# One tile in sixteen takes its source rows from columns copied on chip instead of a row gather

## The chip, the cores and the metric

The kernel runs on one core of a Trainium2 chip. A core has a matrix engine (PE, with its weight loads shown apart as PEld), a vector engine (DVE), a scalar engine (ACT), a general engine (POOL, GpSimd), an engine that only issues transfers (SP, SyncE), and 16 DMA engines. Each engine works through its own list of instructions in order; the order of the five lists is written out by hand here. The metric is the device time of one execution in microseconds (us), the median of several runs.

## The reference

One message-passing layer on a graph: 12,500 nodes with 64 features, 200,000 edges sorted by destination, 32 features per edge.

```python
msg_in = jnp.concatenate([nodes[row], nodes[col], edge_features], axis=-1)
messages = relu(msg_in @ mW1 + mb1) @ mW2 + mb2
aggregated = jax.ops.segment_sum(messages, col, num_segments=nodes.shape[0])
upd_in = jnp.concatenate([nodes, aggregated], axis=-1)
x = _layernorm(x + relu(upd_in @ uW1 + ub1) @ uW2 + ub2)
```

`row` is the source of an edge, in no order; `col` is its destination, in ascending order. All is fp32.

## The kernel before

**Tables.** The product of `msg_in` with `mW1` splits in three: a part of the source node, a part of the destination node and a part of the edge. The first two depend on a node alone, so two tables in DRAM hold them for every node: `tab_a` for sources and `tab_b` (with the bias) for destinations, 128 numbers per node. `chunk_a` and `chunk_b` compute them, most of `tab_a` before the loop.

**Tiles, groups, steps.** The edges are cut in 1563 tiles of 128. Eight tiles are a group (the kernel's `s`, 196 of them), and one pass of the main loop (lines 583 to 622) is one step; two groups share an index `g` and a set of selection matrices. A group's first linear layer is a PSUM bank pair `pc` of 128 x 1024.

**What one step does**, in the program's order, each on its own engine:

- `gather` (line 153) on POOL, for a group up to 14 steps ahead: eight indirect transfers (line 164), one per tile, each fetching 128 rows of `tab_a` by the edges' sources into a row buffer. There are `ROWB` = 14 row buffers; `frees` tells which step's end makes room. The first `XG` = 8 groups, when the table is not complete, gather rows of `x` instead and go through `transpose` and a matmul with `w1a`.
- `windows` (line 213) on SP: eight transfers of 32 consecutive rows of `tab_b` into `rhs`, at a row number that SP reads into a register. Because the edges are sorted, the 128 destinations of a tile lie within 32 nodes.
- `node_part` (line 255): DVE adds the gathered rows to `pc` (line 272), then ACT applies the relu in place (line 273), giving `h`. The add is the last reader of the row buffer; POOL's next gather into this buffer waits for it.
- `collect` (line 283) on PE, for the group before: the messages are summed per destination by a matmul of each tile's `h` with a 32-column selection matrix, into the PSUM tile `sums` at a column from a register (line 298), and likewise the counts of edges (line 303).
- `select`, `counts`, `load`, `loadd` once per two groups: DVE builds the selection matrices `l` (line 192) and `sel` (line 196), ACT makes a bf16 copy of the latter (line 204), SP loads destinations (line 180) and edge features (line 211).
- `edge_part` (line 242) on PE, for the next group: eight matmuls (line 251) of [edge features; selection] with [weights; 32 rows of `tab_b`] into `pc`. They wait for the `rhs` transfers and for the DVE add that frees `pc`, of which there are two.
- every three or four steps a node update of 384 nodes (`close`, `columns`, `carry`, `update`, `residual`, `norm`, `store`).

The order of the DVE's list in a step is: add of line 272, then on every second step lines 190, 192 and 196. ACT's is: relu of line 273, then on every second step line 204.

Of the kernel before, what the change touches and what calls it, by code (L numbers as in the profile page):

```python
# [10 lines left out]
F32 = mybir.dt.float32  # L11
I32 = mybir.dt.int32
AF = mybir.ActivationFunctionType
ALU = mybir.AluOpType
# [3 lines left out]
P = 128  # L18
# [6 lines left out]
SUB = 8  # L25
# [15 lines left out]
EARLY = NCH * P  # L41
GE = 20
BS = 8
UB = 3
NCOL = (-(-N // P) + UB) * P
UW = UB * P
# [16 lines left out]


@with_exitstack
def gnn_kernel(ctx: ExitStack, tc: tile.TileContext, x1T, x, eT, e_rows, src, dst, dst_row, wrow, wnext, whalf,
               mW1, mb1, mW2, mb2, uW1, ub1, uW2, ub2, out):

# [35 lines left out]
    past = const.tile([1, 1], F32, name="past")  # L104
    w1b = const.tile([P, DH], F32, name="w1b")
    b1 = const.tile([P, DH], F32, name="b1")

    sums_s = [const.tile([P, UW], F32, name=f"sums_s{k}") for k in range(2)]
    xw = [const.tile([P, UW], F32, name=f"xw{k}") for k in range(2)]
# [21 lines left out]
    cps = cpool.tile([P, WIN + SUP], F32, name="cps")  # L131
    slot = cps[:, :WIN]
    drc = const.tile([P, NT], F32, name="drc")
    flag_i = const.tile([1, 1], I32, name="flag_i")
    usup = const.tile([1, K], I32, name="usup")
    ustep = const.tile([1, K], I32, name="ustep")
# [4 lines left out]

    rows = ctx.enter_context(tc.tile_pool(name="rows", bufs=ROWB))
    xg = {}

    def frees(s):

# [3 lines left out]
    def tiles(s):  # L150
        return range(s * SUB, min((s + 1) * SUB, NT))

    def gather(s):

        if s >= XG or s % 2 == 0:
            buf = rows.tile([P, SUB, DH], F32, name="xg")
        else:
            buf = xg[s - 1][0]
        if s < XG:
            a = buf.rearrange("p k (b d) -> p (k b) d", d=D)[:, s % 2 * SUB:(s % 2 + 1) * SUB, :]  # L160
        else:
            a = buf.rearrange("p (b k) d -> p k b d", b=2)
        for i, t in enumerate(tiles(s)):
            nc.gpsimd.indirect_dma_start(  # L164
                out=a[:, i, :] if s < XG else a[:, i // 2, i % 2, :], out_offset=None, in_=A[:, :] if s >= XG else x[:, :],
                in_offset=bass.IndirectOffsetOnAxis(ap=src_s[:, t:t + 1], axis=0))
        xg[s] = buf, a

    with tc.tile_pool(name="sup", bufs=2) as sup, tc.tile_pool(name="work", bufs=2) as work, tc.manual_schedule():
# [63 lines left out]
            nc.scalar.copy(xt, pt)  # L233
            xs[s] = xt

        def parts(n):

            if n == SUB:
                return [slice(0, SUB)]
            return [slice(b * SUB // 2, b * SUB // 2 + (n - b + 1) // 2) for b in range(2) if n > b]  # L240

        def edge_part(s):

            n = len(tiles(s))
            g, j = divmod(s, SUP // SUB)
            pc = psum.tile([P, 2, SUB // 2, DH], F32, name="pc")
            for i in range(n):
                k, b = divmod(i, 2)
                q, m = 64 * b, j * SUB // 2 + k

                nc.tensor.matmul(pc[:, b, k, :], L[g][q:q + 64, m, :], rhs[g % 2][q:q + 64, m, :],  # L251
                                 start=s >= XG or k == 0, stop=s >= XG)
            pcs[s] = pc

        def node_part(s):

            n = len(tiles(s))
            pc = pcs.pop(s)
            h = work.tile([P, 2, SUB // 2, DH], F32, name="h")
            if s < XG:  # L260
                xt = xs.pop(s)
                for i in range(n):
                    k, b = divmod(i, 2)
                    q = 64 * b
                    nc.tensor.matmul(pc[:, b, k, :], xt[q:q + 64, k, :], w1a[q:q + 64], start=False,
                                     stop=i + 2 >= n)
                nc.scalar.activation(h, pc, AF.Relu)
            else:
                hf, pf = (t.rearrange("p b k f -> p (b k) f") for t in (h, pc))
                a = xg.pop(s)[0]  # L270
                for m in parts(n):
                    nc.vector.tensor_tensor(hf[:, m], pf[:, m], a[:, m], op=ALU.add)  # L272
                    nc.scalar.activation(hf[:, m], hf[:, m], AF.Relu)  # L273
            hs[s] = h

        def opened(u):
# [37 lines left out]
        def close(u):  # L314

            ps, pn = sums.pop(u)
            nc.scalar.copy(sums_s[u % 2], ps)  # L317
            nc.scalar.copy(xw[u % 2][0:1], pn)

        us = {}  # L320

# [46 lines left out]
            nc.sync.dma_start(out[bass.ds(n0, UW), :].rearrange("(c p) d -> p c d", p=P), o)  # L368


        WCH = 1024

        def relative(a, b):

# [108 lines left out]
        for k, c in enumerate(range(0, NB, NCH)):  # L483
            chunk_a(c)
            if k == 0:
                chunk_b(0, [B0v, Bv])
            if k == 2:

                w0 = wint[:, :GE * SUP]
                nc.vector.tensor_scalar(past, w0[:, GE * SUP - 1:], float(EARLY - WIN), None, op0=ALU.is_gt)  # L490
                nc.vector.tensor_scalar(w0, w0, float(EARLY - WIN), None, op0=ALU.min)
                windows(0)
                windows(1)
            if k == 4:
                relative(0, 8 * SUP)
            if k == 6:
                offsets()
            if k == 9:
                select(0)
                load(0)  # L500
                counts(0)
        columns_of(NCH, nc.sync)

        def rest(s):

            if s == 1:
                relative(8 * SUP, 8 * SUP + WCH)
            elif s == 2:
                relative(8 * SUP + WCH, NT)
# [73 lines left out]
        for s in range(last + 3):  # L583
# [18 lines left out]
            if chunks and s >= BS and chunks[0] < NCH + NB * (s + 1 - BS) / (SUP // SUB * (GE - 1) - BS):  # L602
                if len(chunks) > 1:
                    columns_of(chunks[1], nc.sync)
                chunk_b(chunks.pop(0), [Bv])
            if s + 1 < NSUB:
                if s + 1 < XG:
                    transpose(s + 1)
                edge_part(s + 1)
# [179 lines left out]
```

## Time and profile before

| | |
|---|---|
| median of 3 runs | 2791.69 us |
| lowest, highest | 2774.48 us, 2797.45 us |
| the profiled execution | 2797.45 us, of which its span 2795.7 us |
| POOL busy | 1476.6 us (53%), 1572 instructions |
| PE matmuls busy, weight loads busy | 1650.0 us (59%), 1427.7 us (51%) |
| DVE busy | 553.1 us (20%), 1103 instructions |
| ACT busy | 361.6 us (13%), 534 instructions |
| DMA traffic | 213.70 MB, mean 76 GB/s |
| gathers of `tab_a` by POOL | 1499, of 64 KB each |

A line of the profile's list of groups reads: line, engine, operation, written tile <- read tiles, number | busy us, mean ns of one | idle time of the engine just before them, and what ended it. A line of the timeline reads: start, duration, engine, line, operation, and in brackets the engine's idle time before it and what ended it. "issue" means that the profile shows nothing that was waited for; "remote" that a semaphore was waited for whose writer the profile does not name. SPq is SP's list of transfers.

### The profile page before, as it was taken

What the parts mean: (1) busy time and instruction counts of PE and PEld (TensorE: products, weight loads), DVE (VectorE), ACT (ScalarE), POOL (GpSimd) and SP (SyncE); (2) the same over time, 40 slices, a digit from 0 to 9 for tenths busy, and PEclk for the clock granted to TensorE, in tenths of its full rate; (3) what the DMA queues carried; (4) which work ended last, traced back from release to release, by engine and by line L of the source; (5) the groups of instructions that cost most, each with busy time, mean ns of one, the idle gap of its engine ahead of it and who ended that gap; (6) DMA issues with size and microseconds to landing.
All of it is one profiled execution on the core that took longest, in us unless ns stands there. A gap on an engine that the chain in (4) does not pass through costs nothing. (4 is left out here: it accounts for less than half of the span.)

```text
span 2795.7 us, 34750 instructions
## 1 busy us (share of the span) xinstructions
PE 1650.0 (59%) x9558; PEld 1427.7 (51%) x9558; DVE 553.1 (20%) x1103; ACT 361.6 (13%) x534; POOL 1476.6 (53%) x1572
## 2 busy tenths in 40 slices
PE   1412755555564646655656655656666676675788
PEld 1312654555454545544546544555555555564667
DVE  0200121222111112111211211212122222221233
ACT  0100101101010111111111111111111111111122
POOL 7175445654555655555555564565555555555510
PEclk6555555555555555555555555555555555555566
DMA  3531233333222222222222222222222222222221
GB/s 89 144 90 51 74 84 91 90 93 85 69 75 67 78 67 73 74 72 72 74 73 74 73 75 71 70 77 76 71 76 66 77 75 75 75 78 73 74 69 44
DMA packets 248063, 213.70 MB, mean 76 GB/s; under 512 B 81153, under 2 KB 213143, under 8 KB 247880
## 3 DMA queue, kind: packets, MB, share of 16 engines
q0 software_dynamic: 50016, 100.44, 14.0%
q1 hardware_dynamic: 182310, 100.72, 13.1%
q10 hardware_dynamic: 15554, 10.31, 1.3%
q8 instruction: 90, 1.47, 0.2%
q14 instruction: 93, 0.76, 0.1%
HBM read 192.55 MB, written 18.68 MB: 76 GB/s over the span
## 5 line engine op out<-in xcount | busy, mean ns | idle before, releaser
L164 POOL DMA_INDIRECT xg<-tab_a,src_s x1499 | 1415.0, 944 | 1183.8 <-DVE h L272 440.6
L251 PE MATMUL pc<-rhs,l 64*128 64x128 f32 x3126 | 531.4, 424 | 677.5 <-issue 411.8
L251 PEld LDWEIGHTS pc<-rhs,l 64*128 64x128 f32 x3126 | 432.1, 306 | 733.9 <-issue 629.4
L298 PEld LDWEIGHTS sums<-sel,h 128*128 128x128 f32 x3126 | 637.2, 301 | 206.6 <-issue 199.8
L298 PE MATMUL sums<-sel,h 128*128 128x32 f32 x3126 | 626.8, 366 | 151.7 <-issue 149.8
L272 DVE TENSOR_TENSOR h<-pc,xg 128x1024 f32<-128x1024 f32 x189 | 228.6, 1210 | 954.5 <-remote 319.5
L273 ACT ACTIVATE h<-h 128x1024 f32<-128x1024 f32 x189 | 197.7, 1047 | 598.9 <-DVE h L272 495.3
L196 DVE TENSOR_TENSOR sel<-cps,drc 128x512 f32<-128x512 f32 x98 | 67.3, 686 | 634.6 <-remote 333.4
L192 DVE TENSOR_TENSOR l<-l,cps 128x1024 f32<-128x1024 int32 (+1 forms) x101 | 123.3, 1221 | 206.0 <-DMA l<-in_dst_row 159.6
L204 ACT CAST selb<-sel 128x512 bf16<-128x512 f32 x98 | 60.4, 616 | 667.4 <-DVE sel L196 398.4
L303 PE MATMUL cnt<-selb,one 128*1 128x32 bf16 x1563 | 95.2, 188 | 51.0 <-issue 50.6
L336 ACT ACTIVATE hTu<-pu,ub_s 128x384 f32<-128x384 f32 x54 | 31.3, 580 | 696.0 <-remote 308.5
L344 PE MATMUL py<-ux,xw 128*128 128x64 f32 x324 | 95.5, 384 | 26.7 <-issue 23.1
L303 PEld LDWEIGHTS <-one 128*1 128x1 bf16 x1563 | 62.7, 83 | 89.7 <-issue 77.5
L345 PE MATMUL py<-u,hTu 128*128 128x64 f32 x324 | 93.9, 382 | 21.1 <-issue 20.7
L344 PEld LDWEIGHTS py<-ux,xw 128*128 128x128 f32 x324 | 77.1, 288 | 34.3 <-issue 28.4
L345 PEld LDWEIGHTS py<-u,hTu 128*128 128x128 f32 x324 | 79.8, 297 | 26.0 <-issue 25.5
L408 PE MATMUL pb<-w1a,xl 64*128 64x128 f32 x196 | 30.6, 430 | 99.6 <-DMA xl<-in_x1T 93.2
L333 PE MATMUL pu<-sums_s,w2u 128*128 128x384 f32 x108 | 88.2, 921 | 1.5 <-ACT sums_s L317 1.5
L408 PEld LDWEIGHTS pb<-w1a,xl 64*128 64x128 f32 x196 | 26.2, 311 | 103.7 <-issue 92.8
L334 PE MATMUL pu<-xw,uz 128*128 128x384 f32 x108 | 73.7, 782 | 0.0
L349 DVE BATCH_NORM_STATS2 st<-py 128x6 f32<-128x64 f32 x162 | 26.6, 220 | 237.6 <-PE py L345 120.3
(86 smaller groups left out, 594.3 us busy)
## 6 DMA issues: line engine op xcount, KB each, us to landing
l<-in_dst_row SPq DMA_DIRECT2D x196, 128.0 KB
l<-in_eT SPq DMA_DIRECT2D x196, 128.0 KB
rhs<-tab_b SPq DMA_DIRECT2D x1563, 16.0 KB
xg<-tab_a,src_s POOLq DMA_INDIRECT x1499
tab_b<-tb SPq DMA_DIRECT2D x13, 512.0 KB
tab_a<-tb ACTq DMA_DIRECT2D x12, 512.0 KB
xw<-in_x1T SPq DMA_DIRECT2D x54, 97.5 KB
out<-o SPq DMA_DIRECT2D x54, 96.0 KB
```

The lines of the kernel that those rows point to most:

```text
L164: nc.gpsimd.indirect_dma_start(out=a[:, i, :] if s < XG else a[:, i // 2, i % 2, :], out_offset=None, in_=A[:, :] if s >= XG else x[:, :], ...
L192: nc.vector.tensor_tensor(l[r], l[r].bitcast(I32), node[r].unsqueeze(2).broadcast_to([r.stop - r.start, SUP // 2, P]), op=ALU.is_equal)
L196: nc.vector.tensor_tensor(s[:, :nt], slot.unsqueeze(1).broadcast_to([P, nt, WIN]), drc[:, g * SUP:g * SUP + nt].unsqueeze(2).broadcast_to( ...
L251: nc.tensor.matmul(pc[:, b, k, :], L[g][q:q + 64, m, :], rhs[g % 2][q:q + 64, m, :], start=s >= XG or k == 0, stop=s >= XG)
L272: nc.vector.tensor_tensor(hf[:, m], pf[:, m], a[:, m], op=ALU.add)
L273: nc.scalar.activation(hf[:, m], hf[:, m], AF.Relu)
L298: nc.tensor.matmul(ps[:, bass.ds(ws[i], WIN)], h[:, i % 2, i // 2, :], S[g][:, k0 + i, :], start=False, stop=ends and i == n - 1)
L303: nc.tensor.matmul(pn[:, bass.ds(ws[i], WIN)], one, SB[g][:, k0 + i, :], start=False, stop=ends and i == n - 1)
L333: nc.tensor.matmul(pu, w2u, sums_s[u % 2], start=True, stop=False)
L334: nc.tensor.matmul(pu, uz, xw[u % 2], start=False, stop=True)
L344: nc.tensor.matmul(py[:, i], xw[u % 2][:, i * P:(i + 1) * P], ux, start=True, stop=False)
L345: nc.tensor.matmul(py[:, i], hT[:, i * P:(i + 1) * P], u2, start=False, stop=True)
```

## The change

From group 12 on, in every second group, the last of the eight tiles is no longer gathered. Its source rows of `x` come from a copy of the transposed `x` that is kept in SBUF (`xcol`, features on 64 partitions, one column per node): for each of the tile's 128 edges one column of 64 numbers is copied into a tile `xo`, at a column number read into a register, and one more matmul with `w1a` adds that tile's source part to `pc`. The 128 columns are copied in two consecutive steps, 64 in each: 36 by ACT, 28 by DVE. The DVE's copies are written as an addition of a column of zeros in PSUM. So 91 of the 1499 gathers go; 11,648 column copies come, with as many register instructions, and 91 matmuls. `xcol` is loaded before the loop by seven transfers on SP (3.2 MB), `srow` (the sources, a tile per row) in step 2. In the groups concerned, the DVE add covers seven tiles, and ACT applies the relu of the eighth straight from PSUM.

In the main loop `copies(s)` stands after `select`, `load`, `counts`, `loadd` and `chunk_b` and before `edge_part(s + 1)`; a tile `xo` is filled in an even and the following odd step, and `edge_part` reads it in the step after these.

```diff
+CG = 2
+CF = 6 * CG
+CA = 36
+NCT = -(-(NSUB - CF) // CG)
...
+    xcol = const.tile([P, NB * P], F32, name="xcol")
...
+    srow = const.tile([NCT, P], I32, name="srow")
+    xo = [const.tile([P, P], F32, name=f"xo{k}") for k in range(2)]
...
+    def copied(s):
+        return s >= CF and s % CG == CG - 1 and len(tiles(s)) == SUB
...
-        for i, t in enumerate(tiles(s)):
+        for i, t in enumerate(tiles(s)[:SUB - copied(s)]):
...
+                c = copied(s) and i == n - 1
                 nc.tensor.matmul(pc[:, b, k, :], L[g][q:q + 64, m, :], rhs[g % 2][q:q + 64, m, :],
-                                 start=s >= XG or k == 0, stop=s >= XG)
+                                 start=s >= XG or k == 0, stop=s >= XG and not c)
+                if c:
+                    nc.tensor.matmul(pc[:, b, k, :], xo[s // CG % 2][q:q + 64], w1a[q:q + 64], start=False, stop=True)
...
-                for m in parts(n):
+                for m in parts(n, copied(s)):
                     nc.vector.tensor_tensor(hf[:, m], pf[:, m], a[:, m], op=ALU.add)
                     nc.scalar.activation(hf[:, m], hf[:, m], AF.Relu)
+                if copied(s):
+                    nc.scalar.activation(h[:, 1, SUB // 2 - 1], pc[:, 1, SUB // 2 - 1], AF.Relu)
...
+        def copies(s):
+            t = (s + 2) // CG * CG + CG - 1
+            if t < CF or not t < NSUB or not copied(t):
+                return
+            n = P // CG
+            k = (s + 2) % CG * n
+            r = t // CG - CF // CG
+            to = xo[t // CG % 2]
+            def by_dve(o, i):
+                nc.vector.tensor_tensor(o, i, slot[D:, 0:1], op=ALU.add)
+
+            parts = []
+            for a, b, e, copy in ((k, k + CA // 2, ET.Activation, nc.scalar.copy),
+                                  (k + CA // 2, k + CA, ET.Activation, nc.scalar.copy),
+                                  (k + CA, k + n, ET.DVE, by_dve)):
+                _, v = nc.values_load_multi_w_load_instructions(
+                    srow[r:r + 1, a:b], engines=[e], min_val=0, max_val=N - 1,
+                    skip_runtime_bounds_check_because="sources are node numbers")
+                parts += [(copy, a + i, v[i]) for i in range(b - a)]
+            for copy, i, v in parts:
+                copy(to[D:, i:i + 1], xcol[D:, bass.ds(v, 1)])
...
+        def xload(c):
+            e = min(c + XCH, NB * P)
+            nc.sync.dma_start(xcol[D:, c:e], x1T[1:, c:e])
...
                 counts(0)
+                for c in range(0, NB * P, XCH):
+                    xload(c)
...
                 chunk_b(chunks.pop(0), [Bv])
+            copies(s)
             if s + 1 < NSUB:
```

More of the change, by code (lines that the diff above doesn't have):

```diff
@@ L65, in gnn_kernel @@
 @with_exitstack
-def gnn_kernel(ctx: ExitStack, tc: tile.TileContext, x1T, x, eT, e_rows, src, dst, dst_row, wrow, wnext, whalf,
+def gnn_kernel(ctx: ExitStack, tc: tile.TileContext, x1T, x, eT, e_rows, src, src_row, dst, dst_row, wrow, wnext, whalf,
                mW1, mb1, mW2, mb2, uW1, ub1, uW2, ub2, out):
@@ L234, in transpose, with parts @@
             xs[s] = xt
-        def parts(n):
+        def parts(n, last=False):
             if n == SUB:
-                return [slice(0, SUB)]
+                return [slice(0, SUB - last)]
             return [slice(b * SUB // 2, b * SUB // 2 + (n - b + 1) // 2) for b in range(2) if n > b]
@@ L368, in store @@
             nc.sync.dma_start(out[bass.ds(n0, UW), :].rearrange("(c p) d -> p c d", p=P), o)
+        XCH = 2048
         WCH = 1024
+        def xload(c):
+            e = min(c + XCH, NB * P)
+            nc.sync.dma_start(xcol[D:, c:e], x1T[1:, c:e])
         def relative(a, b):
@@ L508, in rest @@
             elif s == 2:
+                nc.sync.dma_start(srow, src_row[CF * SUB + SUB * CG - 1::SUB * CG, :][:NCT])
                 relative(8 * SUP + WCH, NT)
@@ L771 @@
         "src": sp.reshape(-1, P).T[:, :NT],
+        "src_row": sp.reshape(-1, P),
         "dst": dp[:EPAD].reshape(-1, P).T[:, :NT],
```

## The prediction

> **What bounds the kernel now.** I read the page first, for the engine that is nearest to full. None is: POOL 53%, PE 59%. The groups of instructions show POOL's gathers waiting for the DVE's add, and the DVE in turn waiting for something that is mostly not named.
>
> ```profile
> L164 POOL DMA_INDIRECT xg<-tab_a,src_s x1499 | 1415.0, 944 | 1183.8 <-DVE h L272 440.6
> L272 DVE TENSOR_TENSOR h<-pc,xg 128x1024 f32<-128x1024 f32 x189 | 228.6, 1210 | 954.5 <-remote 319.5
> L196 DVE TENSOR_TENSOR sel<-cps,drc 128x512 f32<-128x512 f32 x98 | 67.3, 686 | 634.6 <-remote 333.4
> ```
>
> Then the windows, for the middle of the loop and for its end, after the last gather (2680.5 us):
>
> ```profile
> 700.00:2100.00 1400.00, 841.04 (x4703) 736.15 (x4703) 267.04 (x490) 177.05 (x250) 788.00 (x837) 0.52 0.27 73
> 2698.00:2780.00 82.00, 82.00 (x593) 68.69 (x591) 31.45 (x85) 24.72 (x43) 0.00 (x0) 0.73 0.22 59
> ```
>
> Columns are the stretch, its length, busy time and count on PE, PEld, DVE, ACT, POOL, the clock, the DMA share and GB/s. In the middle, PE runs 4703 matmuls in 1400 us, 3.4 per us; at the end, with no gathers, 7.2 per us. The clock explains little of this: PE idles for two fifths of the middle. The adds of line 272 start 13.65 us apart per two steps at the end (2705.2, 2718.9, 2732.5), so a step takes 6.8 us there. In the middle it takes 13.46 us (104 adds). So something costs the other engines half their pace while POOL gathers. SP's list shows the same: eight transfers of line 225, first among the 14 buffers' worth of gathers at the start, then near the end.
>
> ```profile
> 154.21 33.07 SPq L225 DMA_DIRECT2D rhs<-tab_b  x8
> 2699.91 3.83 SPq L225 DMA_DIRECT2D rhs<-tab_b  x8
> ```
>
> The timeline shows how such a stretch ends.
>
> ```profile
> 1511.49 0.94 POOL L164 DMA_INDIRECT xg<-tab_a,src_s  x1 [0.30 <-issue]
> 1511.91 0.37 PE L251 MATMUL pc<-rhs,l 64*128 64x128 f32 x1 [2.42 <-issue]
> ...
> 1515.51 0.69 DVE L196 TENSOR_TENSOR sel<-cps,drc 128x512 f32<-128x512 f32 x1 [11.55 <-remote]
> 1516.12 1.22 DVE L272 TENSOR_TENSOR h<-pc,xg 128x1024 f32<-128x1024 f32 x1
> ...
> 1517.60 0.94 POOL L164 DMA_INDIRECT xg<-tab_a,src_s  x1 [5.16 <-DVE h L272]
> ```
>
> POOL had gathered since 1492.8. From 1501 on PE's matmuls come one by one, 0.7 to 2.4 us apart, with nothing to wait for. `sel` needs only the sums of the group before, whose matmuls ended at 1499.4; the trace's semaphore records carry ten of PE's signals of 1499 to 1512 all between 1515.49 and 1515.92. Three us after the last gather everything is let go at once: `sel`, the add, and with the add POOL's next gather. So the loop alternates: POOL gathers for 8 or 16 tiles and PE and SP crawl; then POOL stands still until an add frees a buffer, and PE and SP catch up. In the middle the gathering takes 837 x 1.244 us (944 ns and 0.30 of issue) = 1041 us of 1400, 9.96 us of a step of 13.46; 3.5 us of a step is POOL's standing still.
>
> **The change part by part.** *The gathers that go.* 91 x 1.244 = 113 us of gathering. Since it and the catching up take turns, I count all of it: -113. If the catching up had to make good for the shorter crawl, less; at SP's paces (8 transfers in 33 us against 3.8) the crawl is worth about a ninth of full pace, so this is 13 us, inside the range.
>
> *The copies.* No row shows a column copy with a register; the nearest are these.
>
> ```profile
> L273 ACT ACTIVATE h<-h 128x128 f32<-128x128 f32 x1 | 0.3, 293 | 0.0
> L550 DVE TENSOR_TENSOR mm<-mm,drc 64x1 f32<-64x1 f32 x1 | 0.2, 151 | 0.0
> L351 DVE BATCH_NORM_AGGREGATE mv<-st 128x2 f32<-128x6 f32 x162 | 16.1, 154 | 0.0
> ```
>
> ```profile
> L294 PEldq TENSOR_LOAD <-woff x196: 585/591/1592, 140.0 to 2774.7; - x196
> ...
> L308 PEldq TENSOR_LOAD <-ustep x53: 301/305/459, 639.4 to 2773.9; - x53
> ```
>
> ACT: the relu of 1024 columns takes 1054 ns, that of 128 takes 293, so 0.85 ns a column and 185 ns for an instruction of one. From below, PE's list gives register instruction and matmul at starts 0.12 us apart (eight from 1494.50 to 1495.33). 36 copies are 4.3 to 6.7 us, taken as 5.4, the middle, since ACT's own pairs overlap by 0.1 us in the trace but a dependent register may spoil that. DVE: one of 64 x 1 takes 151 ns; `mv`, back to back, 99 ns from start to start (16.1 / 162). 28 copies are 2.8 to 4.2 us, taken at 0.12 as 3.4. Register loads: 1 register in 0.305 us, 8 in 0.591, so 0.041 for each further: two of 18 on ACT are 2.0 us, one of 28 on DVE 1.4.
>
> The Trainium skill ("Runtime: NRT & Kernel Launch", section Instruction fetch mechanics) speaks against this: a register load costs about 200 ns for each register, even in bulk. By it ACT's 36 registers would be an estimated 7.2 us a step, its sum 14.5 us would be over the step's 13.46, and the kernel about 180 us slower; the row of eight registers in 0.591 us, where the page would have 1.6, disagrees, so I don't use it.
>
> Per step ACT then has 361.6 / 196 = 1.85 us of today plus 7.4 = 9.2 (at most 10.5), DVE 553.1 / 196 = 2.8 plus 4.8 = 7.6 (at most 8.4). Both are below 13.46, so neither is the bound by its sum; what counts is where in the lists the copies stand. On ACT they delay the next relu, behind which PE's sums wait; on the DVE they stand between `sel` and the next add, and POOL waits for the add. Where `sel` runs early, the copies fall in the gathering, which hides them. In 57 of 98 cases (34 remote, 10 by line 298, 13 by line 251) `sel` is itself held; then the add comes 4.8 us later than now. That is 57 x 4.8 = 274 us on the path at most. But PE and SP run at full pace in these 4.8 us, which is more than SP's eight transfers of a step need (3.83); the next add is then not held, and the next standing still is shorter by as much. I take it that nine tenths come back: +25.
>
> *What else.* After the last gather there is no gathering to hide behind: nine copying steps there (the adds after 2682.4, to group 191) would take 9.2 us on ACT instead of 6.8: +2.4 x 9 = +22, between 0 and 33. `xcol`'s seven transfers stand on SP's list ahead of the next groups' windows, at 130 to 146 us, where SP is about to crawl; queued behind them are line 399's and line 225's transfers and with them PE's first groups. 3.2 MB at the 144 GB/s of the page's second slice are 22 us; seven issues alone are 5 (0.71 each, as at 188 us). PE has no work then that lasts longer, but POOL fills its 14 buffers until 251 anyway: +10, from 0 to 35. 91 matmuls of 0.42 us, less 91 eighths of the DVE's add (0.15 each) and a second relu of 0.29: some 50 us of work, spread over engines that idle for 40% and more: 0; without that cover 0.5 us for each concerned step.
>
> Sum: -113 + 25 + 22 + 10 = -56, from 2797.5 of the profiled execution 2741. That one was 5.8 us above the median, so about **2735** with the median before of 2791.7 (my forecast would read -2%). Its bounds are 2680, where nothing but the 113 counts, and 2763, where 85 us of the losses stay.
>
> **The rivals.** *The DVE's copies hold up the gathers* (slower). The add is what starts POOL, and the 4.8 us stand right in front of it in the 57 held cases. For it: POOL's largest waits are for the DVE (440.6 us in 67 waits, and 223.3 in 50 that end with line 190, just after an add). PE's signals are held whether or not PE is ahead, so the time given to PE and SP may not help: what counts is that an add can only fire once in a gathering stretch or after it. Against it: SP's crawl shows that SP is behind, and time is what it lacks. It decides once over 81 us (113 less 32) of the 274 stay, 30%. With 60% staying, -113 + 32 + 164 = +83: 2875 (2820 to 2985).
>
> *ACT and DVE crawl too* (slower). PE and SP, the two that crawl, are the two that run long lists with registers; ACT and DVE would now be such. No row shows either of them do so while POOL gathers. Against it: their own signals pass at once there (the add ends at 1499.69, the relu that waits for it starts at 1499.79, among gathers). At 33.07 us for 32 instructions, ACT would get 9 of its 74 through in the 9.3 us of gathering and need 32 pairs x 0.15 us = 4.9 after them: 9.3 + 4.9 + 1.85 = 16 us a step, +2.6 x 182 = +470, with -113 and +32 about 3180, and from 2950 if they crawl less.
>
> *It comes to nothing*: about 40% of the 274 stays, or ACT's late relu costs as much: 2765 to 2820.
>
> **How the numbers follow.** Forecast 0.42, held gathers 0.30, nothing 0.16, crawl 0.12. Within 1% is 2764 to 2820, about what a measurement of this kernel can tell from no change. Faster 0.42, same 0.16, slower 0.42. The forecast's own range is 2680 to 2763; to hold 8 in 10 the range must also reach over the third case and most of the first rival: 2680 to 2950, which leaves out the crawl and the rival's upper end. Faster and slower are equally likely here; 2735 is the likeliest single case.
>
> **What would show it.** Right: 1408 gathers of `tab_a` of 944 ns; POOL's waits for the DVE no longer in sum than now (664 us); the ACT's column copies at 0.12 to 0.19 us and the DVE's at 0.10 to 0.15, from start to start, also among gathers; a step near 12.9 us in the middle. First rival: adds that follow column copies without a pause, POOL's waits up by 80 us or more, steps with standing still of 8 us and more. Crawl: column copies 0.7 us apart while POOL gathers. Start: the first add of line 272 (318.9 us now) later by 10. The prediction is wrong if the gathering isn't what PE and SP crawl for: then POOL's 113 us are worth nothing.

## The result, and the profile after

The changed kernel takes 2926.0 us (median of 4 runs, 2913.3 to 2943.7), the kernel before 2789.6 in the same runs: 1.050 times as long, with an interval of 1.043 to 1.057. The forecast was 2735, faster; it is slower by 136 us. The profiled execution took 2928.1 us, with a span of 2926.3.

The groups of instructions, the three that answer to those shown before, and the new ones (busy us, mean ns of one, idle time before them and what ended it):

```profile
L176 POOL DMA_INDIRECT xg<-tab_a,src_s x1408 | 1331.7, 946 | 1360.1 <-DVE h L287 583.3
L358 ACT COPY xo<-xcol 64x1 f32 x6552 | 741.7, 188 | 1320.5 <-issue 1312.9
L347 DVE TENSOR_TENSOR xo<-xcol,cps 64x1 f32<-64x1 f32 x5096 | 685.2, 159 | 641.5 <-issue 639.6
...
L287 DVE TENSOR_TENSOR h<-pc,xg 128x1024 f32<-128x1024 f32 (+1 forms) x189 | 216.9, 1148 | 365.7 <-DMA xg<-tab_a,src_s 147.7
...
L208 DVE TENSOR_TENSOR sel<-cps,drc 128x512 f32<-128x512 f32 x98 | 67.0, 684 | 300.5 <-PE sums L315 138.1
```

The 91 gathers are gone (1408 and 64 early ones in place of 1563), and POOL's idle time has grown from 1183.8 to 1360.1 us. Its waits for the DVE (583.3 for the add, 285.1 that end with line 202, just after an add) are 868 us, 204 more than before. DVE's `sel` no longer waits mostly for something unnamed: "remote" is now 117.7 of its 300.5 us, where it was 333.4 of 634.6. The ACT's copies have 1313 us of idle time in front of them that ends with nothing but "issue".

The windows of the middle and of the end, columns as before:

```profile
700.00:2100.00 1400.00, 763.03 (x4457) 668.38 (x4458) 615.10 (x3190) 570.75 (x3811) 695.16 (x736) 0.51 0.25 66
2780.00:2880.00 100.00, 77.54 (x467) 66.91 (x468) 59.57 (x324) 54.18 (x367) 0.00 (x0) 0.57 0.18 48
```

736 gathers in 1400 us where there were 837: with 7.5 tiles a step in place of 8, a step takes 14.3 us (98 adds) and not 13.5. At the end, without gathers, PE runs 4.7 matmuls per us, where it ran 7.2; the adds are 22 us apart per two steps (2819.2, 2841.1, 2863.4), where they were 13.65.

The timeline of ACT shows what its "issue" is (start, time from first to last end, count, idle time before):

```profile
1509.37 0.26 ACT L290 ACTIVATE h<-pc 128x128 f32<-128x128 f32 x1
1514.38 1.20 ACT L358 COPY xo<-xcol 64x1 f32 x11 [4.76 <-issue]
...
1524.48 0.19 ACT L358 COPY xo<-xcol 64x1 f32 x1 [1.21 <-issue]
1525.91 0.19 ACT L358 COPY xo<-xcol 64x1 f32 x1 [1.24 <-issue]
1527.32 0.19 ACT L358 COPY xo<-xcol 64x1 f32 x1 [1.22 <-issue]
1528.71 0.19 ACT L358 COPY xo<-xcol 64x1 f32 x1 [1.20 <-issue]
1530.11 0.99 ACT L358 COPY xo<-xcol 64x1 f32 x9 [1.21 <-issue]
1531.12 1.06 ACT L288 ACTIVATE h<-h 128x1024 f32<-128x1024 f32 x1
...
1536.72 3.42 ACT L358 COPY xo<-xcol 64x1 f32 x33 [4.03 <-issue]
```

Two different things. The 4.76 and 4.03 us ahead of the first copies are register loads. And between 1516 and 1529, while POOL gathers (its gathers of this stretch start at 1508.69 to 1526.86), the copies come one by one, 0.7 to 1.4 us apart; after the last gather nine come 0.10 us apart. That is the crawl that PE and SP already showed: single instructions far apart, with nothing that the profile shows them waiting for. The list of line 353's register loads, and the longest pieces of the chain of waits (start, us, what):

```profile
L353 ACTq TENSOR_LOAD <-srow x364: 16/2237/5321, 358.9 to 2882.6; - x182
L353 DVEq TENSOR_LOAD <-srow x182: 1847/1898/2166, 357.2 to 2879.3; - x182
```

```profile
2816.41 4.04 ACTq L353
2838.38 4.04 ACTq L353
2860.64 4.04 ACTq L353
2882.62 4.04 ACTq L353
```

ACT's two loads of a step are not alike: in order of time the records alternate between about 1.5 and 4.0 us for 18 registers each (medians 1.51 and 4.00), 1004 us in all. The DVE's 28 take 1.9. The 15 longest pieces of the chain are all ACT loads of 4.0 us. The chain reaches back only to 2317 us, so it speaks for the last fifth of the span.

### The profile page after: what moved, and what is told of

It is laid out like the page before. It is cut to its first block, busy times and chain, and to the rows that moved or that the text cites. A ratio compares the mean times of both kernels' runs of the same rounds, so it can differ in the third digit from the quotient of the medians.

```text
span 2926.3 us, 58914 instructions
## 1 busy us (share of the span) xinstructions
PE 1647.8 (56%) x9740; PEld 1433.8 (49%) x9740; DVE 1231.7 (42%) x6199; ACT 1104.9 (38%) x7177; POOL 1393.4 (48%) x1481
## 3 DMA queue, kind: packets, MB, share of 16 engines
q8 instruction: 92, 1.51, 0.2%
## 5 line engine op out<-in xcount | busy, mean ns | idle before, releaser
L176 POOL DMA_INDIRECT xg<-tab_a,src_s x1408 | 1331.7, 946 | 1360.1 <-DVE h L287 583.3
L358 ACT COPY xo<-xcol 64x1 f32 x6552 | 741.7, 188 | 1320.5 <-issue 1312.9
L347 DVE TENSOR_TENSOR xo<-xcol,cps 64x1 f32<-64x1 f32 x5096 | 685.2, 159 | 641.5 <-issue 639.6
L264 PE MATMUL pc<-rhs,l 64*128 64x128 f32 x3126 | 436.6, 430 | 309.7 <-issue 119.1
L264 PEld LDWEIGHTS pc<-rhs,l 64*128 64x128 f32 x3126 | 368.0, 318 | 345.1 <-issue 134.2
L287 DVE TENSOR_TENSOR h<-pc,xg 128x1024 f32<-128x1024 f32 (+1 forms) x189 | 216.9, 1148 | 365.7 <-DMA xg<-tab_a,src_s 147.7
L288 ACT ACTIVATE h<-h 128x1024 f32<-128x1024 f32 (+1 forms) x189 | 187.9, 995 | 114.6 <-DVE h L287 96.0
L318 PE MATMUL cnt<-zero_b 128*1 128x384 bf16 x54 | 25.5, 472 | 357.1 <-ACT xw L335 321.2
L208 DVE TENSOR_TENSOR sel<-cps,drc 128x512 f32<-128x512 f32 x98 | 67.0, 684 | 300.5 <-PE sums L315 138.1
L267 PE MATMUL pc<-w1a,xo 64*128 64x128 f32 x182 | 62.5, 444 | 213.5 <-ACT xo L358 167.8
L267 PEld LDWEIGHTS pc<-w1a,xo 64*128 64x128 f32 x182 | 46.8, 315 | 226.1 <-ACT xo L358 176.1
```

The lines of the kernel that those rows point to most:

```text
L176: nc.gpsimd.indirect_dma_start(out=a[:, i, :] if s < XG else a[:, i // 2, i % 2, :], out_offset=None, in_=A[:, :] if s >= XG else x[:, :], ...
L347: nc.vector.tensor_tensor(o, i, slot[D:, 0:1], op=ALU.add)
L358: copy(to[D:, i:i + 1], xcol[D:, bass.ds(v, 1)])
```

## The experiments

Each group of runs shared runs of the kernel before on its chip, and these chips were of two kinds: on some the kernel before takes 2787 to 2793 us, as in the prediction (groups 1, 4, 5, 6), on others 1985 (groups 2 and 3), with the same program. So every time below stands beside its own time before. The theories were three: the ACT's own list is the cost (its loads above all), the DVE's copies hold the adds up (the first rival), the copies crawl among gathers (the second).

### Group 1, before 2789.8: what the gathers bring, and whose copies cost

`no_copies`:

```diff
-            copies(s)
```

> No column copies and no loads of their column numbers; the 91 gathers stay dropped, the matmul of line 267 reads two tiles set to zero once (so the x part of 91 tiles' sources is left out of the result). What is left of the change is the 91 gathers, xcol's transfers and the matmuls. All theories of the copies say the same here: 2790 - 113 + 10 = 2687 us if my two terms hold. If instead the loop only waits longer after shorter gathering (the time that PE and SP need to catch up does not shrink), 2740 to 2790, and the prediction's first term is wrong as well.

2631.2 us, 0.941 (0.937 to 0.945) of before. The edit is worth 159 us without its copies, not 103. (Where a run leaves copies out, the two tiles `xo` are set to zero once; the diffs here don't show that.)

`act_alone` and `dve_alone` keep one engine's part:

```diff
-                                  (k + CA // 2, k + CA, ET.Activation, nc.scalar.copy),
-                                  (k + CA, k + n, ET.DVE, by_dve)):
+                                  (k + CA // 2, k + CA, ET.Activation, nc.scalar.copy)):
```

> The ACT's 36 copies of a step and their two loads stay; the DVE's 28 and their load are left out (44 percent of the columns stay zero, so part of 91 tiles' x is left out). Theory A, ACT's own list is the cost (in the changed kernel's trace its two loads take 1.5 + 4.0 us, 36 copies 3.6, some 11 us of a step of 14.3, and 0.7 us a copy while POOL gathers): little is won, 2860 us or more. Theory B, the first rival, the DVE's copies hold the adds up: nearly all of the loss goes, 2700 to 2740.

```diff
-            for a, b, e, copy in ((k, k + CA // 2, ET.Activation, nc.scalar.copy),
-                                  (k + CA // 2, k + CA, ET.Activation, nc.scalar.copy),
-                                  (k + CA, k + n, ET.DVE, by_dve)):
+            for a, b, e, copy in ((k + CA, k + n, ET.DVE, by_dve),):
```

> The DVE's 28 copies of a step and their load stay; the ACT's 36 and their two loads are left out (56 percent of the columns stay zero). Theory A (ACT's list): 2700 to 2740, nearly all of the loss goes. Theory B (the DVE's copies in front of the adds): 2860 or more. If each alone gives 2790 to 2850, the loss is shared between them.

ACT alone 3235.1 us (1.159, 1.156 to 1.162), DVE alone 2822.5 (1.013, 1.008 to 1.018). ACT's copies cost 604 us over the run without copies, the DVE's 191, both together 295. So ACT's part is the dear one, where the first rival would have had the DVE's; but the parts don't add up, and no theory had both together cheaper than one alone.

`fixed_columns`:

```diff
-                _, v = nc.values_load_multi_w_load_instructions(
...
-                parts += [(copy, a + i, v[i]) for i in range(b - a)]
+                parts += [(copy, a + i, 97 * r + a + i) for i in range(b - a)]
...
-                copy(to[D:, i:i + 1], xcol[D:, bass.ds(v, 1)])
+                copy(to[D:, i:i + 1], xcol[D:, v:v + 1])
```

> The same 6552 + 5096 copies at the same places, but from columns fixed in the program: no register loads, no register instruction ahead of each copy (the columns copied are not the sources', so 91 tiles get other x rows). ACT's list of a step falls from 11.1 to 5.7 us, the DVE's from 8.3 to 6.4, the instructions by half. If the loads (5.5 us on ACT, 1.85 on DVE) are the main cost: 2720 to 2760. If it is the crawl by the number of instructions: half of the 240 us of loss, about 2800. If it is the copies as such: 2860 or more.

2749.0 us, 0.985 (0.983 to 0.987). Loads and register instructions together are 177 of the 295 us; the copies as such 118. And these copies, which need no register, crawl among gathers too (DVE's timeline; the last gather of POOL's stretch runs from 1509.75 to 1510.70):

```profile
1505.60 1.73 DVE L347 TENSOR_TENSOR xo<-xcol,cps 64x1 f32<-64x1 f32 x22
...
1509.04 0.16 DVE L347 TENSOR_TENSOR xo<-xcol,cps 64x1 f32<-64x1 f32 x1 [1.23 <-issue]
1510.45 0.16 DVE L347 TENSOR_TENSOR xo<-xcol,cps 64x1 f32<-64x1 f32 x1 [1.25 <-DMA xg<-tab_a,src_s]
```

So a register isn't what makes an instruction crawl.

### Group 2, before 1985.0: loads or copies

`loads_once` loads the numbers in the first copying step and keeps them; `loads_mainly` runs every load and 3 of 64 copies; `load_by_load` puts each load's copies right behind it:

```diff
+                if a - k not in kept:
+                    _, kept[a - k] = nc.values_load_multi_w_load_instructions(
...
+                v = kept[a - k]
```

```diff
-            for copy, i, v in parts:
+            for copy, i, v in [parts[0], parts[CA // 2], parts[CA]]:
```

```diff
-                parts += [(copy, a + i, v[i]) for i in range(b - a)]
-            for copy, i, v in parts:
-                copy(to[D:, i:i + 1], xcol[D:, bass.ds(v, 1)])
+                for i in range(b - a):
+                    copy(to[D:, a + i:a + i + 1], xcol[D:, bass.ds(v[i], 1)])
```

> All copies with a register and their register instruction, at their places, but the column numbers are loaded once, in the first copying step, and kept (the later tiles get the first two tiles' columns). 364 - 2 loads on ACT (1004 us busy in the changed kernel) and 182 - 1 on DVE (347 us) go. If the loads are the main cost: 2750 to 2800, near the run with fixed columns (2749). If the pairs of register instruction and copy, which come 0.7 us apart among gathers, are: 2870 or more.

> The reverse: every load as it is, but only the first copy behind each load (3 of 64 a step; the other columns stay zero). If the loads as such cost: 2750 or more. If the copies do, 2640 to 2690, within 2 percent of the run without copies (2631).

> Nothing left out; only the order on ACT is changed: load of 18, its 18 copies, second load, its 18 copies. In the changed kernel the second load, right behind the first, takes 4.0 us and the first 1.5. If the 4.0 comes of two loads in a row, both now take 1.5 and the time falls to 2830 to 2880 (2.5 us of ACT in each of 182 steps, of which some half is on the path). If it comes of the place or the registers, the second still takes 4.0 and the time is 2926 within 1 percent.

`loads_once` 1872.7 us (0.944, 0.942 to 0.945), `loads_mainly` 1875.9 (0.945, 0.944 to 0.947), `load_by_load` 2121.8 (1.070, 1.068 to 1.072). On this kind of chip POOL's gathers of `loads_once` follow each other to the end at 1.249 us, and 91 of them are worth 112 us, the prediction's first term. Loads without copies cost nothing there, nor do copies without loads; with loads of 18 it takes both for ACT to be over POOL's pace. In `load_by_load` the second load still takes 3.94 us (median) though 18 copies lie between the two: the reason isn't that two loads follow each other.

`act_and_pause` is `act_alone` with four adds on the DVE, some 6 us, in the place of its copies:

```diff
+            for i in range(4):
+                nc.vector.tensor_tensor(idle, idle, idle, op=ALU.add)
```

> The kernel with the ACT's copies alone (3235 us, 309 slower than with both), and in the place of the DVE's 28 copies four adds on an unused tile of 1280 columns, some 6 us of DVE time with hardly an instruction (the DVE's columns stay zero). Theory: the DVE's work in front of the add breaks POOL's stretches of gathers into 7 and 8, and in the pauses between them ACT's list catches up; then 2900 to 3000. Otherwise, a late add is only a further loss: 3235 or more.

2181.0 us (1.099, 1.097 to 1.102). It says nothing of its theory, which is of chips where POOL gathers in stretches with pauses between them; and the pause itself lengthened the gathers (see the last section).

### Group 3, before 1984.9: the change on the second kind of chip, and other loads

`change_again` is the changed kernel as it is.

> The changed kernel once more, because the second group of four runs ran on a chip where the kernel before takes 1985 us and not 2790: gathers there stand 1.249 us apart without a pause. On a chip of the first kind: 2926 within 1 percent. On one of the second kind: ACT's list of some 11 us a step (5.5 of it register loads) is longer than POOL's gathering of 7.5 tiles a step (9.4 us), so ACT is the bound and the time is about 2120, as with the loads in another order (2122).

2123.3 us (1.069, 1.067 to 1.071). The change loses 138 us here too, for one plain reason. The chain of waits of this run (share of the span by line), and its timeline of ACT and then of POOL:

```profile
ACTq L353 26%; POOL xg L176 18%; ACT xo L358 12%; PE sums L315 2%; DMA tab_a<-tb 2%; ACT h L288 2%; ACT selb L216 1%; DVE h L287 1%; PE pc L264 1%; DMA xg<-tab_a,src_s 1%; PE pu L373 1%; PE pu L374 1%; ACT hTu L376 1%; DVE o L402 1%; DVEq L353 0%
```

```profile
1508.85 1.10 ACT L358 COPY xo<-xcol 64x1 f32 x10 [4.52 <-issue]
1510.14 2.70 ACT L358 COPY xo<-xcol 64x1 f32 x26 [0.19 <-issue]
...
1514.30 0.61 ACT L216 CAST selb<-sel 128x512 bf16<-128x512 f32 x1
1518.51 3.52 ACT L358 COPY xo<-xcol 64x1 f32 x34 [3.60 <-issue]
```

```profile
1509.64 0.94 POOL L176 DMA_INDIRECT xg<-tab_a,src_s  x1 [0.30 <-issue]
1510.89 0.94 POOL L176 DMA_INDIRECT xg<-tab_a,src_s  x1 [0.30 <-issue]
1512.14 0.94 POOL L176 DMA_INDIRECT xg<-tab_a,src_s  x1 [0.30 <-issue]
```

Nothing crawls: 26 copies run 0.10 us apart in the midst of gathers. But 1.5 + 4.0 us of loads, 3.6 of copies and about 2 of everything else are some 11 us a step on ACT (the adds are 10.65 us apart between 700 and 2100 us), POOL's 7.5 gathers at 1.249 are 9.4, and ACT is the bound.

`half_and_half` has one load of 32 and 32 copies on each engine; `loads_of_nine` four loads on ACT; `one_in_32` takes one tile of each four groups, with one load of 16 and 16 copies on each engine:

```diff
-CA = 36
+CA = 32
...
-            for a, b, e, copy in ((k, k + CA // 2, ET.Activation, nc.scalar.copy),
-                                  (k + CA // 2, k + CA, ET.Activation, nc.scalar.copy),
+            for a, b, e, copy in ((k, k + CA, ET.Activation, nc.scalar.copy),
```

```diff
+            for a, b, e, copy in ((k + 0, k + 9, ET.Activation, nc.scalar.copy),
+                                  (k + 9, k + 18, ET.Activation, nc.scalar.copy),
+                                  (k + 18, k + 27, ET.Activation, nc.scalar.copy),
+                                  (k + 27, k + 36, ET.Activation, nc.scalar.copy),
```

```diff
-CG = 2
+CG = 4
...
-CA = 36
+CA = 16
...
```

> Nothing left out: 32 copies a step on ACT and 32 on the DVE, each with one register load of 32. If one load of 32 takes about 2 us (28 took 1.9), ACT's list is 2.0 + 3.2 + 2.1 = 7.3 us a step and the DVE's 2.0 + 4.1 + 2.8 = 8.9, both under POOL's 9.4. Where the kernel before takes 1985: 1870 to 1900. Where it takes 2790: ACT's sum falls by a third, 2770 to 2850. If a load grows steeply above some number of registers (the 4.0 us of the second 18), ACT takes 10 us or more and the time is 2000 or more and 2880 or more.

> Nothing left out: ACT's 36 numbers in four loads of nine in place of two of 18. Which of them are slow tells what the 4.0 us of the second load is: if it is the second load's place, loads two to four are slow (3 us or more each) and the time rises by 3 percent or more; if it is the number of registers, the last two (from the 19th register on) are slow, with the 5.5 us of the sum and the time of the changed kernel within 1 percent; if it is the length of one load, all four take about 0.6 to 1.0 us and the time falls by 2 percent or more.

> Nothing left out: one tile of each four groups of eight, not of each two, so 43 gathers fewer than before instead of 91, and half the copies a step: 16 on ACT and 16 on the DVE with a load of 16 each. By the first kind's prices, 43/91 of the 159 us that the gathers bring (75) less half of what the copies cost with fewer loads (295/2, less the second load's 2.5 us in 182 steps of which some half counts): 2760 to 2830, so no gain. Where the kernel before takes 1985 and POOL is the bound: 1985 - 43 x 1.249 = 1931.

`half_and_half` 1874.5 us (0.944, 0.943 to 0.946): the whole 112 us. `one_in_32` 1932.8 (0.974, 0.972 to 0.975), 52 us for 43 gathers. `loads_of_nine` 2362.3 (1.190, 1.187 to 1.193). The last one's list of loads (minimum, median, maximum in ns):

```profile
L355 ACTq TENSOR_LOAD <-srow x728: 777/1987/3245, 157.4 to 2311.9; - x182
L355 DVEq TENSOR_LOAD <-srow x182: 1847/1901/2153, 155.6 to 2305.1; - x182
```

In order of time a step's four take 0.80, 2.00, 2.00 and 1.99 us (medians): the first 0.09 us a register, the others 0.22. They start 0, 36, 72 and 108 bytes into the step's part of the row; the DVE's loads, at 1.9 us for 28, start at 144.

### Group 4, before 2792.3: where the second load starts, and the same on the first kind of chip

`sixteen_and_twenty`:

```diff
-            for a, b, e, copy in ((k, k + CA // 2, ET.Activation, nc.scalar.copy),
-                                  (k + CA // 2, k + CA, ET.Activation, nc.scalar.copy),
+            for a, b, e, copy in ((k, k + 16, ET.Activation, nc.scalar.copy),
+                                  (k + 16, k + CA, ET.Activation, nc.scalar.copy),
```

> Nothing left out: ACT's two loads are of 16 and 20 registers in place of 18 and 18, so that the second one starts 64 bytes into the row and not 72. So far every slow load (0.22 us a register) started 36, 72 or 108 bytes after the first, every fast one (0.065 a register: ACT's first, the DVE's at 144 bytes, those at 128) at a multiple of 16 bytes. Theory alignment: the second load takes about 1.3 us, ACT's list falls from 11.1 to 8.1 us a step: 1870 to 1890 where the kernel before takes 1985, 2760 to 2850 where it takes 2790. Theory second load on ACT, wherever it starts: 4.4 us, and 2123 or 2926 within 1 percent.

```profile
L353 ACTq TENSOR_LOAD <-srow x364: 1007/1232/1545, 356.8 to 2732.0; - x182
```

2779.1 us (0.994, 0.991 to 0.997). All 364 loads are now between 1.0 and 1.55 us; a second load of 20 takes 1.29 where one of 18 took 4.00. With the loads of nine, this settles it: what counts is where the load starts. This one edit, two numbers in the source, is worth 147 us (2926 to 2779) on chips of the first kind.

`half_and_half` and `loads_once` again:

> 32 copies and one load of 32 on each of ACT and DVE, which took 1874.5 us where the kernel before takes 1985. Where it takes 2790, ACT's list of 7.3 us a step in place of 11.1 and a crawl of 64 pairs as before: 2770 to 2850. If the crawl is the larger part of the loss there, 2880 or more.

> All copies with registers that are loaded once (the later tiles get the first two tiles' columns). Where the kernel before takes 1985: 1873 again. Where it takes 2790: if the loads are the main cost there too, 2750 to 2800; if the pairs of register instruction and copy among gathers are, 2870 or more.

`half_and_half` 2846.4 us (1.021, 1.014 to 1.028), `loads_once` 2813.4 (1.009, 1.006 to 1.012). Without any load after the first step the kernel is 113 us faster than with loads of 18 and 18, and yet 34 slower than with loads of 16 and 20: the time does not follow ACT's load by itself here. The trace of `half_and_half` on this chip shows what else it follows (DVE and POOL):

```profile
1513.24 0.42 DVE L347 TENSOR_TENSOR xo<-xcol,cps 64x1 f32<-64x1 f32 x3 [1.24 <-issue]
1513.92 1.23 DVE L287 TENSOR_TENSOR h<-pc,xg 128x1024 f32<-128x1024 f32 x1 [0.27 <-remote]
1515.42 0.94 POOL L176 DMA_INDIRECT xg<-tab_a,src_s  x1 [3.86 <-DVE cps L202]
```

The DVE's copies crawl, the add follows the last one at once, and POOL has stood waiting for the add. That is the first rival's sign. Of the 131 adds that come behind copies in the DVE's list, 125 start within 0.5 us of the last copy here, and pauses that such adds end are 485 of the 860 us that POOL stands still (in pauses above 1 us). In the changed kernel it is 26 of 131 adds, and 92 of 918 us.

### Group 5, before 2787.2: the rest, ACT's copies or the DVE's

`act_alone_aligned` is `act_alone` with loads of 16 and 20:

```diff
+            for a, b, e, copy in ((k, k + 16, ET.Activation, nc.scalar.copy),
+                                  (k + 16, k + CA, ET.Activation, nc.scalar.copy)):
```

`copies_before_select` has all copies and these loads, and in the step:

```diff
+            copies(s)
             if j == 0 and g + 1 < NSUP:
                 select(g + 1)
...
-            copies(s)
```

> The ACT's 36 copies alone, with loads of 16 and 20 (the DVE's 28 columns stay zero). With both loads slow the ACT's copies alone took 3235 us and both engines' 2926. Where the kernel before takes 2790: if the slow load is what made ACT's part dear, 2650 to 2740, and the DVE's copies in front of the add (2822 alone) are most of what is left of the loss. If ACT's copies crawl among gathers whatever its loads take, 2850 or more. Where the kernel before takes 1985: 1873, POOL's gathers alone being the bound.

> Nothing left out: the kernel with loads of 16 and 20, and the copies of a step issued before the selection and not after it, so that on the DVE they stand right behind an add and in front of a sel that waits for PE anyway, on ACT in front of selb. Where the kernel before takes 2790: if the DVE's copies cost because they follow a held sel and delay the next add, 2680 to 2740; if they cost by crawling, wherever they stand, 2779 within 1 percent; if selb's lateness on ACT holds PE, 2820 or more. Where it takes 1985: 1873.

ACT alone 3031.6 us (1.087, 1.081 to 1.093), copies ahead of the selection 2852.5 (1.024, 1.018 to 1.028). The first is 400 us over the run without copies, with loads of 2.3 us a step, near the 2.0 of the prediction. What it waits for, in its timeline:

```profile
1513.34 0.19 ACT L357 COPY xo<-xcol 64x1 f32 x1 [1.25 <-issue]
1514.72 0.19 ACT L357 COPY xo<-xcol 64x1 f32 x1 [1.20 <-issue]
1515.43 0.49 ACT L357 COPY xo<-xcol 64x1 f32 x4 [0.52 <-issue]
1515.94 1.06 ACT L288 ACTIVATE h<-h 128x1024 f32<-128x1024 f32 x1
1515.97 0.50 PEld L267 LDWEIGHTS pc<-w1a,xo 64*128 64x128 f32 x2 [15.37 <-ACT xo L357]
...
1516.80 1.09 DVE L287 TENSOR_TENSOR h<-pc,xg 128x896 f32<-128x896 f32 x1 [7.03 <-PE pc L267]
...
1518.16 0.95 POOL L176 DMA_INDIRECT xg<-tab_a,src_s  x1 [5.62 <-DVE h L287]
```

This is the second rival at work: ACT's copies trickle through the gathers, PE stands 15.4 us for the last of them with the weight load of the matmul that needs `xo` (360.6 us in 31 such waits), the add waits for that matmul, and POOL for the add.

`copies_before_select` is 73 us slower than with the copies behind the selection, but it doesn't decide about the first rival. The edit moved ACT's copies too, and it put the selection behind all copies; the edge features, which SP loads into the same tile after line 204, then come late, and PE's matmuls wait for them:

```profile
PE pc L264 <- DMA l<-in_eT: 219.1, 46, 11.1
```

With the copies behind the selection (`sixteen_and_twenty`) PE has no such wait; the run without copies has 144 us of it and is fast, so what it costs is not shown.

### Group 6, before 2792.8: why ACT's copies alone cost more than both engines'

`act_alone_aligned`, and ahead of its copies:

```diff
+            for i in range(8):
+                nc.vector.tensor_tensor(idle, slot.unsqueeze(1).broadcast_to([P, SUP, WIN]),
+                                        drc[:, :SUP].unsqueeze(2).broadcast_to([P, SUP, WIN]), op=ALU.is_equal)
```

> The ACT's 36 copies alone with loads of 16 and 20 (3032 us; with the DVE's copies beside them 2779), and in the place of the DVE's 28 copies eight comparisons of 128 x 512 of the kind of sel (0.69 us each, 5.5 us, into a tile that nobody reads; the DVE's columns stay zero). Where the kernel before takes 2790: if the DVE's copies help by keeping the adds apart, so that POOL gathers in stretches of 7 and 8 and ACT gets its list through in between, 2740 to 2850 and hardly a stretch of 15; if what helps is something else in these copies, 3030 or more. Where it takes 1985, POOL is the bound and the run says nothing of this: about 1873.

3033.4 us (1.087, 1.082 to 1.093): a DVE that is busy for as long changes nothing in the time. But the pause didn't make the short stretches that it was to make either (22 of 15 gathers among 76 in the middle), so whether these are the cause isn't settled by it. What helps is at least not the time that the DVE spends there. Why 28 copies on the DVE make ACT's 36 cheaper stays open.

## Why the prediction was wrong

The sum of the runs, on chips where before takes about 2790: -159 for what the change takes away, +148 for its copies with two aligned loads on ACT (2631 to 2779), +147 for the second load as it is (2779 to 2926); together +136.

**The step that failed** is the term of the register loads: "two of 18 on ACT are 2.0 us". They take 5.5 us. The rule of 0.305 us and 0.041 for each further register came from loads of 1 and 8 registers, and the loads of eight all start at multiples of 32 bytes; the second load of 18 starts 72 bytes into its step's part of the row, and such loads cost 0.22 us a register. With it "9.2 (at most 10.5)" us a step on ACT were 11, and "neither is the bound by its sum" fell where no gathers are (the end) and on chips of the second kind altogether. The run with loads of 16 and 20 shows the size: with loads of 2.3 us, near the price that I had assumed, the change is 0.6% faster than before, which the prediction called no change (within 1%), and 44 us from the forecast. So 147 of the 192 us between -56 and +136 are this term. How a load's time becomes the kernel's isn't simple, though: without any loads the kernel is 34 us slower than with aligned ones.

**The Trainium skill's rule** that I set aside ("Runtime: NRT & Kernel Launch", section Instruction fetch mechanics: about 200 ns a register, even in bulk) is near the unaligned loads (18 in 4.00, 9 in 2.00 us: 0.22 each) and far from the aligned loads (32 in 2.02, 28 in 1.90 us: under 0.07). Neither the page nor my rows held both; by the page alone the estimate was "about 180 us slower", closer than mine.

**The other terms were off as well, and made up for each other in part** (-56 for the gathers and the start together, +101 for the copies). The 91 gathers: -113, measured -112 where POOL gathers without pause, but -159 with the start in it where PE and SP crawl, so there it was worth more than the gathers' own time, not less. The copies: +25 in front of the adds and +22 at the end against +148. Here the mechanism was wrong too. I had the copies at full pace "among gathers" and put the risk into the DVE's place ahead of the add; instead ACT's and the DVE's copies crawl, as the rival said to which I gave 0.12, with its own mark ("column copies 0.7 us apart while POOL gathers") in the trace. The reason against it, that a relu starts 0.1 us after its add among gathers, was no evidence: that relu was one instruction and not a long list. The rival's own reason, lists with registers, isn't it either, since copies from constant columns crawl. Its price, 3180, was too high, because a list does not crawl from its first instruction: beside gathers ACT ran 24 copies in 2.7 us (at 1518.7 in the run of ACT's copies alone with aligned loads), and only then by ones, twos and threes, where I had let 9 of 74 instructions through in a whole stretch. Only the runs with ACT's copies alone came near it (3032 and 3235), and they leave the DVE's copies out.

**The first rival** gave 2875 and a range that holds the result, but not the mechanism: POOL's waits for the DVE did rise by 204 us, but its main sign is rare: 26 of the 131 adds behind copies follow them without a pause, the gathers that these start had waited 92 of POOL's 918 us, and pauses of 8 us and more are 23, where before had 26. So the range held the result for another reason, which is luck. In other versions the rival is at work: in 485 of 860 us with 32 copies on each engine, and in 160 of 813 us with the DVE's copies alone, which cost 191 us. There it is one thing with the second rival, since the copies that stand in front of the add crawl.

**At the end**, +22 was to come from nine steps of 9.2 us; they take 11 with loads of 18 and 18 and 8.65 with loads of 16 and 20 (2649.1 to 2735.6 for ten), so the step's working was sound and its load was not. The end after the last gather grew by 37.5 us (114.3 to 151.8), with loads of 16 and 20 by 14.3. **At the start** the first add came at 320.7, 1.8 us later and not 10. The copies' own paces, 0.10 us on ACT and 0.13 on the DVE outside the crawl, were at or under the bounds taken.

The fastest version depends on the chip. Where before takes 2790, loads of 16 and 20 beat both kernels, by 0.6% only; where it takes 1985, one load of 32 on each engine does, by 5.6%. (Versions that leave something out don't count here.) Loads of 16 and 20 weren't tried there.

## What to carry to other kernels

Price an instruction from rows that match it in everything the hardware might look at, its start address too; a slope through two sizes of another instruction is an estimate, and its upper end belongs in the sum's bounds. When some engines crawl in a phase, assume that a list of hundreds of short instructions added to any other engine will crawl in it too, until a row shows a long list that doesn't. And split a tuned edit's price with the cheapest variants (part left out, constants for registers, numbers loaded once) before arguing about where it stands.

## What the runs showed of the hardware

- A load of registers from on-chip memory costs by where it starts. Starts counted from the step's part of the row, at 0, 64 or 128 bytes: 9 in 0.80, 16 in 1.04, 18 in 1.50, 20 in 1.29 and 32 in 2.02 us on ACT; at 144 bytes 28 in 1.90 us on the DVE. At 36, 72 or 108 bytes: 9 in 2.00 and 18 in 4.00 us on ACT. All of it fits one reading to about 0.15 us: from a start at a multiple of 16 bytes, four registers come in 0.25 us, and what is left over, or everything from another start, one by one in 0.22. So 20 aligned ones (five times 0.25) are faster than 18 (four times 0.25, twice 0.22). The two rows of before, 0.59 for 8 and 0.31 for 1, from which I drew a slope, are 0.09 us above it. That it is read in such portions is inferred from the durations alone.
- The same program took 2790 us on some chips and 1985 on others. By the changed kernel's traces, gathers take 0.95 us on both; what differs is that after a first burst the instructions of the other engines come 0.7 us or more apart among gathers on the one kind, and at full pace on the other. The traces don't show why.
- Adds of the DVE on on-chip memory alone (both operands and result, 1280 columns) lengthen the gathers beside them, to 1.22 us and more; comparisons with an operand in PSUM, 0.69 us each, do not. The first run was on a chip of the second kind, the second on one of the first; but on the second kind, too, gathers beside `sel` and beside the DVE's copies, which have one operand in PSUM, take 0.944 us (`change_again`). The gathers' groups of the run with four such adds and of the one with eight such comparisons:

```profile
L177 POOL DMA_INDIRECT xg<-tab_a,src_s x1408 | 1634.3, 1161 | 432.5 <-issue 405.8
```

```profile
L177 POOL DMA_INDIRECT xg<-tab_a,src_s x1408 | 1332.7, 947 | 1461.2 <-DVE h L288 743.0
```

- With a constant column a DVE copy of 64 x 1 starts every 0.072 us outside the crawl, with a register every 0.129.
